# Last layer in pairs of source blocks with clamps on two engines, and another order of the heads' products at the borders of units

## The chip, the core and the metric

The kernel runs on one core of a Trainium2 chip. The metric is device time in microseconds for one execution of the whole program, the median over several runs. TensorE (PE), VectorE (DVE), ScalarE (ACT), GpSimd (POOL) and the DMA queues of SyncE (SP) work side by side and wait for each other through semaphores.

## The reference

Four graph layers run one after the other on x (4096 nodes x 64 features) with one dense 0/1 adjacency matrix (4096 x 4096). Each takes `h = max(layernorm(x), 0)` and adds its result to x.

```python
# layer 0: 6 spatial and 2 intent heads (32 wide), then one output head over their concatenation
e = leaky_relu(f1[:, :, None] + f2[:, None, :], 0.2)          # per head, 4096 x 4096
h_s = elu(softmax(where(adj > 0, e, -9e15)) @ Wh)             # masked attention
# layer 1: hyperbolic attention over neighbours; layer 2: mean of neighbours, W, relu, l2 norm
# layer 3: the last 100 neighbours of each row, halved from one to the one before it
support = h @ weight
mask = adj != 0
rank = cumsum(mask, axis=1);  deg = rank[:, -1:]
k = minimum(deg, 100);  pos = rank - (deg - k)
w = mask * where(pos > 0, 0.5 ** (k - pos), 0.0)
out = w @ support + bias
```

## The kernel before

**Shape of the work.** The adjacency is kept transposed, sources on the 128 partitions and targets along the free axis, so a matrix product with 128 sources (a *block*, 32 of them) adds its part to the sums of many targets. A PSUM bank holds 128 x 512 float32, and most sums are one bank wide. A scheduler orders each engine's instructions from the program's order, its dependences and hints such as `issue_after`.

**The heads (L1443 on).** Targets come in two halves (`hf`) of 2048, and for each half the eight heads (`hd`) are worked through: 16 *units*. The exponential of the leaky sum factors into a source part and a target part once it is known on which side of the leaky relu's corner an edge lies. So a unit needs sign masks, not exponentials. For each pair of blocks `split_edges` makes `st`, the sign of source plus target (one 128x2048 pass per block, most on ACT at L1205, every few on DVE at L1199), then `B = st & edges` (DVE, L1211), and in some pairs `C = B ^ edges` (DVE, L1219); where C is not made, the product with the edges less that with B stands for it.

`add_up` (L1541) multiplies values of 32 columns by four stretches of 512 targets, each landing on its own quarter of the 128 partitions of an accumulator. A spatial head has these accumulators:

- accB: the high half of the values on side B, and accL: their low half, scaled up by LO;
- accD: the denominators;
- accC: the values on the other side.

accB and accC alternate between two pools from one unit to the next, so the next unit's can be started while the last one's are read. accL and accD have one bank each. The two intent heads have no accL; three parts of their values all go to accB. In every pair PE does block by block accB, accL, accD, then accC.

At the end of a unit its sums are evacuated to `ev`: accD by DVE (L1657), accB by ACT (L1658), accC by ACT (L1659), and for spatial heads DVE adds accL/LO (L1661). The rest of the unit's end (`finish_unit`: transposes, division by denominators, elu) is issued at the second pair of the next unit.

**The last layer (L2723 on).** The targets come in four units `u` of 1024. Exponents of the weights come from a product: for each block, `pv` collects a first product with `late` (32 rows deep: how many neighbours lie in later blocks), and a second with `tri` (neighbours within the block, from the fp8 mask `m3`). A relu of `pv` written as int16, read again as bf16 bits, is the weight itself: the clamp (ACT, L2768, 128x1024 in one instruction, `w3b` with three buffers). The products with the support (`sacc`, L2733) of a block come after the `pv` products of the next one. `pv` takes two banks and has two buffers.

Unit 0 is interleaved with the end of the layer before it (four calls of `layer2_group`), whose results are its `SS`, block by block. At a unit's end the two sums are copied out (L2778), turned back by PE (L2783), and added to bias and x (L2791, L2792).

**The check.** The fast form of the kernel is valid for an adjacency of zeros and ones. So every value of it is looked at once: 64 calls of `count_odd` load 128x2048 float32 (1 MB, `raw`, two buffers, on SP's queue) and count the odd ones in one DVE pass (L955). 16 of the 64 are called in the last layer, at every block with `j % 8 == 4`, to be issued after the last `valued`, the last group of the layer before. SP's queue carries the loads of `m3` (512 KB, three buffers) as well.

Of the kernel before, what the change touches and what calls it, by code (L numbers as in the profile page):

```python
# [24 lines left out]
P = 128  # L25
# [810 lines left out]
def kernel(  # L836
# [111 lines left out]

        return col.unsqueeze(2).to_broadcast([P, col.shape[1], width])

    def count_odd(pool, c):

        raw = pool.tile([P, HW], F32, name="raw", tag="raw", bufs=2)
        nc.sync.dma_start(raw, adjT[c % NB * P : (c % NB + 1) * P, c // NB * HW : (c // NB + 1) * HW])
        nc.vector.scalar_tensor_tensor(  # L955
            raw, raw, 0.0, raw, ALU.is_gt, ALU.not_equal, accum_out=bad[:, c : c + 1]
        )
# [83 lines left out]
    with ExitStack() as l0:  # L1041
# [403 lines left out]
        with ExitStack() as ha:  # L1445
# [34 lines left out]
            for hf in range(2):  # L1480
# [9 lines left out]
                for hd in range(NH):  # L1490
# [61 lines left out]
                    for j0 in range(0, NB, 2):  # L1552
                        q = j0 // JT
                        t0 = j0 % JT
                        if spatial:
                            whole = j0 // 2 % 3 > 0
                        else:
                            whole = j0 // 2 % (5 if hf else 2) == 1
                        edges = mres[q][:, t0 : t0 + 2, :]
                        B, C = split_edges(  # L1560
                            epool,
                            srow,
                            nt[:, j0 : j0 + 2, hd],
                            edges,
                            j0 + hd * NB,
                            HEAD_STEPS[not spatial],
                            not whole,
                            3,
                        )
                        if whole:  # L1570
                            C = edges.bitcast(F8)
                        for i, j in enumerate(range(j0, j0 + 2)):
                            for n, (acc, y) in enumerate(parts):
                                sums = add_up(
                                    acc,
                                    y[:, j],
                                    lambda k, i=i: B[:, i, k * G : (k + 1) * G],
                                    start=j == 0 and (n == 0 or acc is not parts[n - 1][0]),
                                    stop=j == NB - 1 and (acc is not accB or n == len(parts) - 2 - spatial),
                                )  # L1580
                        for i, j in enumerate(range(j0, j0 + 2)):
                            for c in range(2):
                                cs = slice(c * O, (c + 1) * O)
                                add_up(
                                    accC,
                                    yc[:, j, cs],
                                    lambda k, i=i: C[:, i, k * G : (k + 1) * G],
                                    start=j == 0 and c == 0,
                                    stop=False,
                                )  # L1590
                                if whole:
                                    add_up(
                                        accC,
                                        ycn[:, j, cs],
                                        lambda k, i=i: B[:, i, k * G : (k + 1) * G],
                                        start=False,
                                        stop=False,
                                    )
                            if first:
                                with behind(sums):  # L1600
                                    add_up(
                                        dm,
                                        YD[:, j].rearrange("p c h -> p (c h)"),
                                        lambda k, q=q, j=j: mres[q].bitcast(F8)[
                                            :, j % JT, k * G : (k + 1) * G
                                        ],
                                        start=(j == 0),
                                        stop=(j == NB - 1),
                                    )
                        if hf == 0 and hd > 0 and j0 % (NB // 2) == 8 and later:  # L1610
                            transfers_after(B.bitcast(U8)[0:1, 0, 0:4], *later.pop(0))
                        if hf == 0 and first and j0 // 2 < NB // 4:
                            with behind(sums, *done_at):
                                other_products(j0 // 2)
                        if hf == 0 and first and j0 == NB // 2:
                            load_products(zt, hd + 1)
                        if j0 >= (NB // 2 + 4 if first else NB // 2 - 4):
                            with behind(*done_at):
                                for _ in range(2 if first else 1):
                                    next(coming, None)  # L1620
                        if j0 == 2 and pending:
                            pending()
                            pending = None
# [23 lines left out]
                    for c in range(2):  # L1647
                        for k in range(NS):
# [5 lines left out]
                                stop=c == 1,  # L1654
                            )
                    ev = by_g
                    nc.vector.tensor_copy(ev[:, 0, :], accD)  # L1657
                    nc.scalar.copy(ev[:, 1, :], accB)  # L1658
                    nc.scalar.copy(ev[:, 2, :], accC)  # L1659
                    if spatial:  # L1660
                        nc.vector.scalar_tensor_tensor(  # L1661
                            ev[:, 1, :], accL, 1.0 / LO, ev[:, 1, :], ALU.mult, ALU.add
                        )

                    def finish_unit(hf=hf, hd=hd, ev=ev, fme=fme):
                        wh = wn[:, hf * HB : (hf + 1) * HB, hd]
# [851 lines left out]
    def layers_fast(es, wide, *sums):  # L2518
# [75 lines left out]
        with not_before_nodes():  # L2594
# [25 lines left out]
            nc.vector.tensor_scalar(w3, w3, Q3[0:D], VAL, ALU.mult, ALU.mult)  # L2620
            fold_3 = lp.tile([P, D], F32, name="fold_3f")
            nc.vector.tensor_scalar(fold_3, fold_h, M3, 2.0**27 / VAL, ALU.mult, ALU.mult)
        late = lp.tile([P, 2, G], BF16, name="late")

        def layer2_group(b0, part, deg):

# [47 lines left out]
        with tc.tile_pool(name="ps_nacc", bufs=6, space=PSUM) as ps_acc:  # L2674
            for hf in range(2):
# [44 lines left out]
                pl = ps.tile([P, G], F32, name="plate", tag="misc")  # L2720
                nc.tensor.matmul(pl, lhsT=lat, rhs=cnt16[:, hf], start=True, stop=True)
                nc.vector.tensor_scalar(late[:, hf], pl, VBITS, None, ALU.min)


        ps_acc = es.enter_context(tc.tile_pool(name="ps_sacc", bufs=2, space=PSUM))
        ps_v = es.enter_context(tc.tile_pool(name="ps_v", bufs=2, space=PSUM))
        for u in range(4):
            hs = slice((u % 2) * HO2, (u % 2 + 1) * HO2)
            accs = [ps_acc.tile([P, G], F32, name="sacc", tag="sacc") for _ in range(NK)]

            def add_up(j, w):
                for k in range(NK):
                    nc.tensor.matmul(  # L2733
                        accs[k],
                        lhsT=SS[:, j].rearrange("p s d -> p (s d)"),
                        rhs=w[:, k * G : (k + 1) * G].bitcast(BF16),
                        start=(j == 0),
                        stop=(j == NB - 1),
                    )

            last = None
            for q in range(NQ):
                m = work.tile([P, JT, HO2], U8, name="m3", tag="m3", bufs=3)
                nc.sync.dma_start(m, mask_d[q][u // 2][:, :, hs])
                for t in range(JT):
                    j = q * JT + t

                    pv = ps_v.tile([P, HO2], F32, name="pv", tag="pv")
                    for k in range(NK):
                        r = ((u % 2) * NK + k) * O  # L2750
                        nc.tensor.matmul(  # L2751
                            pv[:, k * G : (k + 1) * G],
                            lhsT=blk[r : r + O, j, :],
                            rhs=late[r : r + O, u // 2, :],
                            start=True,
                            stop=False,
                        )
                    for k in range(NK):
                        nc.tensor.matmul(  # L2759
                            pv[:, k * G : (k + 1) * G],  # L2760
                            lhsT=tri,
                            rhs=m[:, t, k * G : (k + 1) * G].bitcast(F8),
                            start=False,
                            stop=True,
                        )

                    w = work.tile([P, HO2], I16, name="w3b", tag="w3b", bufs=3)
                    nc.scalar.activation(w, pv, AF.Relu)  # L2768
                    if j % 8 == 4:
                        with tc.issue_after(valued[-1].ins):  # L2770
                            count_odd(work, next(todo))
                    if last is not None:
                        add_up(*last)
                    last = (j, w)
            add_up(*last)
            ev = work.tile([P, NK, G], F32, name="ev3", tag="ev3")
            for k in range(NK):
# [110 lines left out]
```

## Time and profile before

| | |
|---|---|
| median of 3 runs | 2023.15 us (2019.92 to 2024.01) |
| the profiled execution | 2021.7 us |
| its span in the profile | 2019.9 us |
| mean granted TensorE clock | 0.941 |
| heads' stage | about 54 to 930 us |
| ends of the last layer's units (first copy of sums) | 1876.9, 1921.3, 1965.3, 2009.5 us |

The profile is of one execution. A row of the groups reads: line, engine, operation, output from inputs, shapes and count; then busy time, mean ns of one, and the engine's idle time just ahead of them with what ended it. A wait row reads: engine, what waited and its line, what it waited for and its line; then the sum, the number of times, and the longest. PEld is the weight load of TensorE. The clock is the share of full speed that TensorE was granted.

### The profile page before, as it was taken

The numbers are of one execution on the slowest core, as the hardware profiler recorded it, in microseconds if no ns is written. First come the engines' busy times: TensorE is split into PE (matmuls) and PEld (weight loads), VectorE is DVE, ScalarE is ACT, GpSimd is POOL, SyncE is SP. The second block draws the span as 40 slices with busy tenths as digits, with TensorE's granted clock in tenths as the row PEclk, the third lists the DMA queues.
The fourth block names the chain that finished last, engine by engine and source line by source line (L and its number), as shares of the span: only waits on it lengthen the run. The fifth ranks groups of instructions, "written<-read, shape, count | busy, mean of one in ns | idle before, by whom it ended". The sixth has DMA issues, their size and how long they took to land. (4 is left out here: it accounts for less than half of the span.)

```text
span 2019.9 us, 44190 instructions
## 1 busy us (share of the span) xinstructions
PE 1810.5 (90%) x19340; PEld 818.8 (41%) x19340; DVE 1534.4 (76%) x2239; ACT 1474.5 (73%) x1439; POOL 83.4 (4%) x125
## 2 busy tenths in 40 slices
PE   5889989999999999996699958999999985899998
PEld 3444445444444444444244432333333333454332
DVE  6779988998789879996778768888878788533530
ACT  3768888899789888993789857777777743227676
POOL 2000100100000000001011100000000000000000
PEclk8999999999999999997799968999999997889999
DMA  8945564424311111103355415444344336312752
GB/s 112 183 113 100 101 101 65 154 117 172 111 49 49 49 49 54 54 2 96 111 177 194 157 48 199 142 146 153 123 142 150 114 121 221 125 63 73 280 199 65
DMA packets 117016, 239.05 MB, mean 118 GB/s; under 512 B 11062, under 2 KB 84006, under 8 KB 102054
## 3 DMA queue, kind: packets, MB, share of 16 engines
q1 hardware_dynamic: 101996, 192.95, 28.4%
q0 software_dynamic: 14816, 43.18, 11.9%
q8 instruction: 153, 2.51, 0.5%
q14 instruction: 51, 0.42, 0.1%
HBM read 245.37 MB, written 49.46 MB: 146 GB/s over the span
## 5 line engine op out<-in xcount | busy, mean ns | idle before, releaser
L1205 ACT ACTIVATE st<-srow,nt 128x2048 int8<-128x2048 f32 x352 | 682.8, 1994 | 78.4 <-DVE B L1211 77.5
L1211 DVE TENSOR_TENSOR B<-st,mres 128x1024 int32<-128x1024 int32 x256 | 311.7, 1220 | 68.0 <-PE accC L1541 43.5
L1541 PE MATMUL accB<-B,ybh 128*32 128x512 fp8e4 x3072 | 338.7, 384 | 15.6 <-DVE B L1211 15.6
L1541 PE MATMUL accD<-B,ybh 128*32 128x512 fp8e4 x2048 | 301.3, 387 | 21.9 <-DVE h L1657 21.9
L1541 PEld LDWEIGHTS <-ybh 128*32 128x32 bf16 (+1 forms) x6656 | 197.0, 98 | 237.7 <-issue 75.9
L1541 PE MATMUL accC<-B,ycn 128*32 128x512 fp8e4 x2272 | 267.8, 381 | 1.2 <-issue 1.2
L1541 PE MATMUL accC<-mres,ych 128*32 128x512 fp8e4 x2272 | 267.7, 381 | 0.0
L1541 PE MATMUL accL<-B,ybh 128*32 128x512 fp8e4 x1536 | 220.4, 390 | 4.6 <-DVE h L1661 4.5
L1541 PEld LDWEIGHTS <-ych 128*32 128x32 f16 x4096 | 168.7, 98 | 114.5 <-issue 9.1
L1199 DVE TENSOR_SCALAR st<-srow,nt 128x2048 uint8<-128x2048 f32 x160 | 205.4, 1284 | 2.5
L2336 PE MATMUL accj<-sg,who 128*64 128x512 f32 (+1 forms) x512 | 196.6, 614 | 6.5 <-DVE sg L2329 6.1
L2336 PE MATMUL acci<-sg,who 128*64 128x512 f32 (+1 forms) x512 | 196.7, 614 | 0.0
L955 DVE SCALAR_TENSOR_TENSOR raw<-raw 128x2048 f32<-128x2048 f32 x64 | 146.1, 2285 | 33.0 <-DMA raw<-in_adj_dram 32.8
L2292 ACT ACTIVATE yt<-pu,consts 128x512 f32<-128x512 f32 x144 | 98.6, 686 | 98.0 <-PE pu L2291 97.9
L2281 ACT ACTIVATE sg<-pl,rb 128x512 f32<-128x512 f32 x256 | 160.7, 678 | 8.0 <-PE pl L2276 4.9
L2768 ACT ACTIVATE w3b<-pv 128x1024 int16<-128x1024 f32 x128 | 130.9, 1023 | 42.7 <-PE pv L2759 41.2
L1205 ACT ACTIVATE st<-srowo,nto 128x1024 int8<-128x1024 f32 x128 | 138.1, 1137 | 16.4 <-DVE B L1211 14.0
L1541 PE MATMUL accC<-C,ych 128*32 128x512 fp8e4 x1824 | 146.3, 389 | 1.0 <-DVE C L1219 1.0
L1219 DVE TENSOR_TENSOR C<-B,mres 128x1024 int32<-128x1024 int32 x114 | 139.5, 1225 | 3.6
L1541 PEld LDWEIGHTS <-ycn 128*32 128x32 f16 x2272 | 107.7, 97 | 64.2 <-issue 3.6
L2329 DVE SCALAR_TENSOR_TENSOR sg<-pf,sg 128x512 f32<-128x512 f32 x112 | 72.1, 685 | 38.8 <-PE pf L2326 38.8
L2270 PE MATMUL pl<-nm,noid 128*128 128x512 fp8e4 x256 | 82.3, 393 | 13.8 <-ACT sg L2281 12.9
(497 smaller groups left out, 2676.1 us busy)
## 6 DMA issues: line engine op xcount, KB each, us to landing
raw<-in_adj_dram SPq DMA_DIRECT2D x64, 1024.0 KB, 6.2
mo<-edges SPq DMA_DIRECT2D x32, 512.0 KB, 3.9
noedge<-nmo POOLq DMA_DIRECT2D x32, 512.0 KB, 4.1
nm<-noedge SPq DMA_DIRECT2D x64, 256.0 KB, 3.0
m<-edges SPq DMA_DIRECT2D x16, 1024.0 KB, 4.8
m<-edges SPq DMA_DIRECT2D x32, 512.0 KB, 4.9
srow<-srow_d SPq DMA_DIRECT2D x15, 1024.0 KB, 6.8
mres<-in_adj_dram POOLq DMA_DIRECT2D x8, 1024.0 KB, 36.1
```

The lines of the kernel that those rows point to most:

```text
L955: nc.vector.scalar_tensor_tensor(raw, raw, 0.0, raw, ALU.is_gt, ALU.not_equal, accum_out=bad[:, c : c + 1])
L1199: nc.vector.tensor_scalar(st[:, i, :].bitcast(U8), srow, negs[:, i : i + 1], EDGE, ALU.is_gt, ALU.mult)
L1205: nc.scalar.activation(st[:, i, :], srow, AF.Sign, bias=negs[:, i : i + 1], scale=-1.0)
L1211: nc.vector.tensor_tensor(B.bitcast(I32), st.bitcast(I32), edges.bitcast(I32), ALU.bitwise_and)
L1219: nc.vector.tensor_tensor(C.bitcast(I32), B.bitcast(I32), edges.bitcast(I32), ALU.bitwise_xor)
L1541: ins = nc.tensor.matmul(acc[k * O : (k + 1) * O, :], lhsT=values, rhs=moving(k), start=start, stop=stop,)
L2270: nc.tensor.matmul(pl, lhsT=noid, rhs=nm[:, b, :].bitcast(F8), start=True, stop=False)
L2281: nc.scalar.activation(sg[:, b0 + k, :], pl, AF.Sigmoid, bias=rb[:, j : j + 1], scale=1.0)
L2292: nc.scalar.activation(far[gi, gj][:, b, :], pu, AF.Sigmoid, bias=nb_t, scale=2.0 * DIST_K / (DIST_S * DIST_S),)
L2329: nc.vector.scalar_tensor_tensor(v[:, t, :], pf, F_K3, v[:, t, :], ALU.add, ALU.mult)
L2336: nc.tensor.matmul(acc[r : r + n, :], lhsT=XQ[:, src, cols], rhs=w, start=start, stop=stop)
L2768: nc.scalar.activation(w, pv, AF.Relu)
```

## The change

Two parts, in two stages that don't touch each other.

In the heads, a unit other than the very first multiplies its first pair's accB products first, then accC's, and only then accL's and accD's. The last pair does accL and accD for both blocks first, then accB. When a spatial head is evacuated, DVE writes accL/LO to `ev`, copies accD, and adds accB to `ev`; ACT copies accC only. Intent heads are evacuated as before, by the same instructions.

In the last layer two blocks are worked as a pair. The four `late` products of a pair lie on four different row groups of PE: the second block's use `late_x`, a copy of `late` with the two halves of the partitions exchanged (two more DVE passes per half). `pv` becomes four tiles of one bank, with four buffers. The clamp becomes four 128x512 instructions: those with k == 0 on DVE and those with k == 1 on ACT, but in every fourth pair (`j0 % 8 == 4`), which calls the check, all four are on ACT. `w3b` holds a pair and has the pool's own number of buffers. The check is split: its load is now issued one check ahead (`load_rows`), and `check_rows` is called in its old place. The support products of a pair follow the `pv` products of the next pair.

```diff
-    def count_odd(pool, c):
+    def load_rows(pool, c):
         raw = pool.tile([P, HW], F32, name="raw", tag="raw", bufs=2)
         nc.sync.dma_start(raw, adjT[c % NB * P : (c % NB + 1) * P, c // NB * HW : (c // NB + 1) * HW])
+        return raw, c
+    def count_odd(pool, c):
+        check_rows(*load_rows(pool, c))
+    def check_rows(raw, c):
         nc.vector.scalar_tensor_tensor(
             raw, raw, 0.0, raw, ALU.is_gt, ALU.not_equal, accum_out=bad[:, c : c + 1]
         )
...
-                        for i, j in enumerate(range(j0, j0 + 2)):
-                            for n, (acc, y) in enumerate(parts):
-                                sums = add_up(
...
+                        def inside(of_b):
+                            for i, j in enumerate(range(j0, j0 + 2)):
+                                for n, (acc, y) in enumerate(parts):
+                                    if (acc is accB) not in of_b:
+                                        continue
+                                    ins = add_up(
...
+                        if j0 == NB - 2:
+                            inside([False])
+                            sums = inside([True])
+                        elif j0 == 0 and not first:
+                            sums = inside([True])
+                        else:
+                            sums = inside([True, False])
...
+                        if j0 == 0 and not first:
+                            inside([False])
...
                     ev = by_g
+                    if spatial:
+                        nc.vector.tensor_scalar(ev[:, 1, :], accL, 1.0 / LO, None, ALU.mult)
                     nc.vector.tensor_copy(ev[:, 0, :], accD)
-                    nc.scalar.copy(ev[:, 1, :], accB)
+                    if spatial:
+                        nc.vector.tensor_tensor(ev[:, 1, :], ev[:, 1, :], accB, ALU.add)
+                    else:
+                        nc.scalar.copy(ev[:, 1, :], accB)
                     nc.scalar.copy(ev[:, 2, :], accC)
-                    if spatial:
-                        nc.vector.scalar_tensor_tensor(
-                            ev[:, 1, :], accL, 1.0 / LO, ev[:, 1, :], ALU.mult, ALU.add
-                        )
...
                 nc.vector.tensor_scalar(late[:, hf], pl, VBITS, None, ALU.min)
+                for lo, hi in ((slice(0, D), slice(D, P)), (slice(D, P), slice(0, D))):
+                    nc.vector.tensor_scalar(late_x[lo, hf], pl[hi], VBITS, None, ALU.min)
...
-        ps_v = es.enter_context(tc.tile_pool(name="ps_v", bufs=2, space=PSUM))
+        ps_v = es.enter_context(tc.tile_pool(name="ps_v", bufs=4, space=PSUM))
+        rows = load_rows(work, next(todo))
...
-                for t in range(JT):
-                    j = q * JT + t
-                    pv = ps_v.tile([P, HO2], F32, name="pv", tag="pv")
+                for t0 in range(0, JT, 2):
+                    j0 = q * JT + t0
+                    both = [(i, k) for i in range(2) for k in range(NK)]
+                    pvs = {ik: ps_v.tile([P, G], F32, name="pv", tag="pv") for ik in both}
+                    for i, k in both:
+                        r = ((u + i) % 2 * NK + k) * O
                         nc.tensor.matmul(
-                            pv[:, k * G : (k + 1) * G],
-                            lhsT=blk[r : r + O, j, :],
-                            rhs=late[r : r + O, u // 2, :],
+                            pvs[i, k],
+                            lhsT=blk[r : r + O, j0 + i, :],
+                            rhs=(late, late_x)[i][r : r + O, u // 2, :],
...
-                    w = work.tile([P, HO2], I16, name="w3b", tag="w3b", bufs=3)
-                    nc.scalar.activation(w, pv, AF.Relu)
-                    if j % 8 == 4:
+                    w = work.tile([P, 2, HO2], I16, name="w3b", tag="w3b")
+                    for i, k in both:
+                        wk = w[:, i, k * G : (k + 1) * G]
+                        if k == 0 and j0 % 8 != 4:
+                            nc.vector.tensor_scalar(wk, pvs[i, k], 0.0, None, ALU.max)
+                        else:
+                            nc.scalar.activation(wk, pvs[i, k], AF.Relu)
+                    if j0 % 8 == 4:
                         with tc.issue_after(valued[-1].ins):
-                            count_odd(work, next(todo))
+                            check_rows(*rows)
+                            if (u, j0) != (3, NB - 4):
+                                rows = load_rows(work, next(todo))
                     if last is not None:
                         add_up(*last)
-                    last = (j, w)
+                    last = (j0, w)
```

## The prediction

> **What bounds the kernel now.** I read the page's busy table first, then the waits and a timeline of a unit border in the heads' stage, then busy time by stretches, and last the waits of the last layer.
>
> ```profile
> span 2019.9 us, 44190 instructions
> PE 1810.5 (90%) x19340; PEld 818.8 (41%) x19340; DVE 1534.4 (76%) x2239; ACT 1474.5 (73%) x1439; POOL 83.4 (4%) x125
> ```
>
> TensorE is busy 90% of the span, so a gain must be idle PE time, half-clock PE time, or fewer PE passes. The heads run from about 54 to 930 us in 16 units of 52 to 59 us. Waits there (120 to 960 us), each row with its total, count and longest:
>
> ```profile
> DVE B L1211 <- PE accC L1541: 33.5, 35, 2.2
> PE accD L1541 <- DVE h L1657: 21.9, 11, 3.9
> DVE B L1211 <- ACT st L1205: 17.5, 32, 1.7
> PE accL L1541 <- DVE h L1661: 4.5, 5, 3.3
> ```
>
> PE's largest wait, 21.9 us, is for the evacuation copy of accD at a unit's border. The other two rows say that DVE itself mostly waits for PE or ACT, not for its own work. One border, from the timeline (start, duration):
>
> ```profile
> 296.68 1.22 DVE L1211 TENSOR_TENSOR B<-st,mres 128x1024 int32<-128x1024 int32 x1
> 297.94 1.28 DVE L1199 TENSOR_SCALAR st<-srow,nt 128x2048 uint8<-128x2048 f32 x1
> 299.14 0.68 DVE L1657 COPY h<-accD 128x512 f32<-128x512 f32 x1
> 299.88 0.39 PE L1541 MATMUL accD<-B,ybh 128*32 128x512 fp8e4 x2 [2.21 <-DVE h L1657]
> 299.94 0.69 DVE L1661 SCALAR_TENSOR_TENSOR h<-accL,h 128x512 f32<-128x512 f32 x1
> 300.68 0.62 PE L1541 MATMUL accL<-B,ybh 128*32 128x512 fp8e4 x4 [0.41 <-DVE h L1661]
> ```
>
> accB and accC have two buffers each, accL and accD one. PE starts the next unit with one accB product and then stands, since DVE has a sign step of 1.28 us ahead of the copy. Stretches (busy of PE, PEld, DVE, ACT, POOL; PE clock; DMA share; GB/s):
>
> ```profile
> 300.00:304.00 4.00, 3.59 (x38) 1.47 (x39) 3.93 (x4) 4.00 (x3) 0.00 (x0) 0.57 0.18 74
> 780.00:830.00 50.00, 48.70 (x868) 24.01 (x860) 47.38 (x50) 45.30 (x28) 0.00 (x0) 1.00 0.15 55
> 1880.00:1921.00 41.00, 40.91 (x192) 13.26 (x192) 21.03 (x21) 30.70 (x30) 1.57 (x2) 1.00 0.90 323
> ```
>
> After the border the granted clock is 0.57 for 4 us: the stall is paid a second time. In the second half of the heads (780 to 830) DVE is busy 47.4 of 50 us, so what PE gains there DVE can take back. In the last layer PE is busy 40.9 of 41 us, and the DMA share is 0.90. The groups by line there (1880 to 2009 us: busy, mean ns, idle before), and one wait (1830 to 2010 us):
>
> ```profile
> L2768 ACT ACTIVATE w3b<-pv 128x1024 int16<-128x1024 f32 x94 | 96.2, 1023 | 31.6 <-PE pv L2759 31.6
> L2778 DVE COPY ev<-sacc 128x512 f32<-128x512 f32 x2 | 1.4, 688 | 18.9 <-PE sacc L2733 18.9
> L2778 ACT COPY ev<-sacc 128x512 f32<-128x512 f32 x2 | 1.2, 586 | 0.9 <-PE sacc L2733 0.9
> ```
>
> ```profile
> DVE raw L955 <- DMA raw<-in_adj_dram: 29.1, 13, 5.3
> ```
>
> The clamp waits for PE, never the other way; DVE only does checks (16 between 1873 and 1946 us), waits for their transfers, and nobody waits for it.
>
> **The change, heads.** Every unit but the first starts with accB, then accC, and touches accL and accD last; a unit's last pair finishes accL and accD first. For 12 of 16 units (spatial heads) DVE scales accL out by itself, copies accD, and adds accB, where ACT copied accB and DVE added accL. In the changed program's DVE order the two copies stand ahead of the next sign step: the copy comes 1.28 us earlier. On PE the accB products (2 blocks x 4 matmuls) take about 0.43 us and those of accC 0.86 us by the timeline's 0.215 us per four column groups, so accL is needed some 1.1 us later than accD was. The 2.2 us stall at 299 becomes 0 to 0.5 us.
>
> Stalls over all borders, read one by one on PE (3.9 + 1.9, 3.6, 3.3, 2.6, 2.2, 2.8, 0.8, 1.1, 1.1, 3.0, 1.1, 1.7 us), sum to some 26 to 28 us, of which about 24 lie at spatial borders. Half-clock stretches that follow them (191 to 198 us lose 3.4 us, 136 to 144 another 3.4, six others 1.7 each) lose 13.6 us. The ceiling is 40 us. Added: DVE has one more 128x512 PSUM pass per spatial unit, 0.69 us (row L1661, 685 ns), 12 x 0.69 = 8.2 us; ACT loses a copy of 0.56 us. DVE's own instructions in a first-half unit add up to about 49 us (46.0 busy of 50 in 180 to 230), PE's to 47; so once the stall is gone DVE's work sets the unit. I take 2 to 2.4 us for each of 6 first-half borders and 3 us in all for the second half: about -15 us. Bounds: -4 (DVE takes back all but the clock losses at the two worst borders) to -26 (stalls go, clock returns at half of them).
>
> A rule is weighed here. The trace has half clock after PE idled 2.2 us at 299 and 3.6 us at 192, and none after 2.8 us at 411. The Trainium skill, "TensorE: Matmul & The Clock Gate" (Part 1), says the clock halves after an idle window of about 3.4 us, free-running. By a strict 3.4 us the border clock losses would be some 5 us of the 13.6; by the trace, shorter stalls count, with luck in them. I use the trace for what is won, and for new gaps below.
>
> **The change, last layer.** Per pair of blocks before: 2 x (late 0.32 + tri 0.44 + sacc 0.43 + switches 0.09) = 2.57 us; late products start every 1.285 us (1849.10, 1850.39, 1851.68). After: four late products on four row groups at once, 0.32 (before, two on two groups take 0.32), 8 full products x 0.2135 = 1.71, switches 0.09: 2.12 us. If that set the pace, 64 pairs x 0.45 = 29 us would go, 21 in the three units that are not interleaved with the previous layer.
>
> It won't set it alone. The clamp is now four 128x512 instructions. Their prices are in the rows for sacc, the same shape from PSUM: DVE 0.69, ACT 0.59. In three of four pairs DVE has two (1.38), ACT two (1.17); with the products before it and the release after it, the loop through one PSUM bank and DVE is about 0.2 + 1.38 + 0.08 + 0.32 + 0.21 = 2.2 us. In the fourth pair (the check's) ACT has all four: 4 x 0.59 + 0.6 of the same round trip = 2.95. Four pairs: 3 x 2.2 + 2.95 = 9.6 against 10.28 us: -0.7 per four pairs, -2.6 per undisturbed unit.
>
> A rule speaks on this split: "ScalarE: Activation LUTs" (Rules for kernel authors) sends relu and max to VectorE, up to three times faster in bf16. Here the operand is float32 in PSUM, and the rows say 0.69 on DVE against 0.59 on ACT. By the rule a DVE clamp would take about 0.2, and the pair would fall to 2.12 and PE's bound; by the rows it is the slower half. I take the rows.
>
> The checks: 16 of 2.29 us on DVE each, fed by 1 MB transfers that land after 7.6 us (median here; 5.2 at best) through two buffers. Before, DVE waited 29.1 us for them at no cost. Now DVE's program has 2 checks ahead of unit 1, 10 within it, 4 in unit 2, none in unit 3, each with the clamps of later pairs queued behind it. A clamp that stands behind a waiting check stops PE two pairs later, and SP's queue holds mask loads (m3) behind raw loads that wait for an earlier check. With a check every 4.4 to 4.7 us as now, 10 checks alone take 44 to 47 us, against a unit of 44.2 (ends of units 1876.9, 1921.3, 1965.3, 2009.5). A part of the 24 clamps x 0.69 = 16.6 us fits into the waits (13 waits, 29.1 us: 2.2 each), the rest adds. Unit 1: 48 to 56, say +7; unit 2 with 4 checks -1; unit 3 -2.6; unit 0, bound by the chain of the previous layer's four groups (14.8 us each), 0 to +1.5. late_x costs 2 x 2 DVE passes of 64x512 at 0.69 (row of late, 691 ns): 2.8 us, about half on the path, at the start and the end of unit 0, +1.3. No row shows PE gaps of 2 to 4 us there; after such gaps in the heads the clock halved, 1.7 us each: 0 to +5, I take +0.5. Sum: about +5, bounds -12 (checks find their way between clamps) to +13.
>
> **Sum.** -15 + 5 = -10 us. The profiled execution took 2021.7 us (span 2019.9), 1.5 below the median of 2023.15; against the median that is 2013.
>
> **The rivals.**
> 1. The checks decide (slower). One mechanism: in unit 1 DVE meets each check before its transfer landed, and nothing overlaps: 10 x (2.29 + 2.24 wait) + 16.6 of clamps = 62 us against 44, +18, with half clock after some of the gaps +3. With a heads' gain at its low end, -4, that is +17: 2040. It decides as soon as unit 1 is longer than some 59 us, or than 48 if the heads bring only -4. For it: the 29.1 us row and the DMA share of 0.90. Against: clamps do fill waits, and raw loads are issued one check ahead.
> 2. Both parts pay (faster). Heads -28 with most of the clock, last layer -12: 1983. For it: PE is the last wait everywhere. Against: DVE at 47.4 of 50.
> 3. The heads' stall changes its name: PE waits for B where it waited for accD, DVE's 8.2 us more are paid, heads -4, last layer +3: 2022, no change. For it: the DVE rows of 780 to 880 us. Against: DVE waited 33.5 us for PE over the stage.
> 4. The scheduler leaves the DVE copies behind the sign step in some units: heads -8, as in 3 otherwise. The written order speaks against it.
>
> **How the numbers follow.** A few runs tell no change to about 0.2%, 4 us. Forecast 0.55 (2003 to 2019, at 2013), rival 2 0.17 (1978 to 2000), rivals 3 and 4 0.15 (2016 to 2027), rival 1 0.13 (2027 to 2045). The range 1995 to 2027 leaves out about 0.2. Faster 0.73, same 0.13, slower 0.14.
>
> **What would show it.** Heads: the waits of PE for accD and accL, 26 us together, fall below 8; no half clock at 191 or 300 us; DVE B <- PE accC shrinks and PE accB <- DVE B grows if DVE takes over. Last layer: DVE waits on raw within unit 1, PE on w3b there; unit 1 above 46 us, unit 3 near 41. I am wrong if unit 1 is no longer than before, or if the heads' units keep their length.

## The result, and the profile after

The changed kernel took 2025.12 us in the median of 22 runs (2021.37 to 2033.89), the kernel before 2023.09 beside it: a ratio of 1.0012, interval 1.0002 to 1.0023. The forecast was 2013. Its profiled execution has a span of 2023.3 us against 2019.9. The page's first rows, of the changed kernel:

```profile
span 2023.3 us, 44268 instructions
PE 1803.8 (89%) x19323; PEld 821.9 (41%) x19340; DVE 1602.9 (79%) x2351; ACT 1426.4 (71%) x1459; POOL 83.4 (4%) x125
```

PE is busy 6.7 us less in a span that is 3.4 us longer: it waits some 10 us more than before. The heads' stage ends (last accD copy) at 931.7 us instead of 929.1. In the last layer, from the last `pnf` product of the layer before (1855.1 us, before 1858.1) to the last unit's first copy of sums (2012.2, before 2009.5), it takes 157.1 us instead of 151.4: +5.7.

**Heads.** The waits of the changed kernel from 120 to 960 us, some of its rows:

```profile
DVE B L1218 <- PE accC L1548: 33.2, 39, 2.2
PE pt L1699 <- DVE rd L1716: 30.9, 13, 3.5
DVE B L1218 <- ACT st L1212: 14.3, 27, 1.7
PE accL L1548 <- DVE h L1680: 3.1, 3, 1.5
```

and accD's row in the groups:

```profile
L1548 PE MATMUL accD<-B,ybh 128*32 128x512 fp8e4 x2048 | 288.8, 387 | 1.6 <-DVE h L1681 1.6
```

The waits for accD and accL fell from 26.4 to 4.7 us, as meant. A new one, 22.8 us longer than it was, stands at the top of PE's: `pt <- rd`, 30.9 us, against 8.1 before:

```profile
PE pt L1676 <- DVE rd L1693: 8.1, 8, 2.1
```

These are the third set of transposes in `finish_unit`. The `misc` tiles of PSUM have two buffers; the third `pt` takes the first one's, and must wait until DVE's sums `rd` have read it. The border at 299 us of before, in the changed kernel (timeline of DVE and PE; start and duration):

```profile
294.60 0.68 DVE L1680 TENSOR_SCALAR h<-accL 128x512 f32<-128x512 f32 x1
295.20 0.68 DVE L1681 COPY h<-accD 128x512 f32<-128x512 f32 x1
295.80 0.68 DVE L1683 TENSOR_TENSOR h<-h,accB 128x512 f32<-128x512 f32 x1
...
299.93 1.22 DVE L1218 TENSOR_TENSOR B<-st,mres 128x1024 int32<-128x1024 int32 x1
301.18 1.23 DVE L1226 TENSOR_TENSOR C<-B,mres 128x1024 int32<-128x1024 int32 x1
302.32 1.22 DVE L1218 TENSOR_TENSOR B<-st,mres 128x1024 int32<-128x1024 int32 x1
303.45 0.20 DVE L1714 TENSOR_REDUCE rd<-pt 128x16 f32<-128x48 f32 x1
```
```profile
295.94 0.40 PE L1548 MATMUL accD<-B,ybh 128*32 128x512 fp8e4 x4 [0.19 <-DVE h L1681]
...
299.72 1.09 PE L1699 MATMUL pt<-ident,h 128*128 128x128 f32 x8
...
303.92 0.63 PE L1699 MATMUL pt<-ident,h 128*128 128x128 f32 x4 [2.35 <-DVE rd L1716]
```

The border itself costs PE 0.19 us instead of 2.6. Four microseconds later PE has made two sets of transposes, runs a few products on, and stands 2.35 us at the third set: DVE's queue has B, C and B ahead of the sum that frees the tile. Over the whole stage PE's idle time did not shrink, and its mean clock did not rise. Here is the stretch from the first to the last accD copy, before and after (columns as in the prediction):

```profile
135.06:929.13 794.07, 752.51 (x12799) 373.89 (x12802) 707.62 (x778) 684.95 (x420) 25.51 (x33) 0.98 0.30 78
134.77:931.71 796.94, 750.85 (x12769) 370.47 (x12773) 713.70 (x790) 680.65 (x407) 25.52 (x33) 0.97 0.30 78
```

PE is idle 41.6 us of it before and 46.1 after.

**Last layer.** The first copies of sums of the units are at 1873.9, 1925.4, 1971.0 and 2012.2 us: units 1 to 3 take 51.4, 45.7 and 41.2 us, against 44.4, 44.0 and 44.2. DVE in unit 1 and at the start of unit 2, where clamps (L2798) stand behind checks (L962):

```profile
1894.60 2.28 DVE L962 SCALAR_TENSOR_TENSOR raw<-raw 128x2048 f32<-128x2048 f32 x1
1896.81 0.08 DVE L962 DVE_READ_ACCUMULATOR raw<-raw 128x1 f32 x1
1898.41 2.29 DVE L962 SCALAR_TENSOR_TENSOR raw<-raw 128x2048 f32<-128x2048 f32 x1 [1.51 <-DMA raw<-in_adj_dram]
1900.62 0.08 DVE L962 DVE_READ_ACCUMULATOR raw<-raw 128x1 f32 x1
1900.62 1.28 DVE L2798 TENSOR_SCALAR w3b<-pv 128x512 int16<-128x512 f32 x2
```
```profile
1939.61 2.29 DVE L962 SCALAR_TENSOR_TENSOR raw<-raw 128x2048 f32<-128x2048 f32 x1 [2.73 <-DMA raw<-in_adj_dram]
1941.83 0.08 DVE L962 DVE_READ_ACCUMULATOR raw<-raw 128x1 f32 x1
1941.83 1.28 DVE L2798 TENSOR_SCALAR w3b<-pv 128x512 int16<-128x512 f32 x2
```
```profile
1942.56 0.38 PE L2778 MATMUL pv<-late_x,LDf 32*128 32x512 bf16 x1 [2.76 <-DVE w3b L2798]
```

Two checks in a row and a wait for the second one's transfer hold DVE from 1894.6 to 1900.6; at 1939.6 a wait of 2.73 us and a check come before the next clamp, and PE stands 2.76 us.

### The profile page after: what moved, and what is told of

Read it like the earlier page. It is cut to its first block, busy times and chain, and to the rows that moved or that the text cites. A ratio compares the mean times of both kernels' runs of the same rounds, so it can differ in the third digit from the quotient of the medians.

```text
span 2023.3 us, 44268 instructions
## 1 busy us (share of the span) xinstructions
PE 1803.8 (89%) x19323; PEld 821.9 (41%) x19340; DVE 1602.9 (79%) x2351; ACT 1426.4 (71%) x1459; POOL 83.4 (4%) x125
## 5 line engine op out<-in xcount | busy, mean ns | idle before, releaser
L1548 PE MATMUL accB<-B,ybh 128*32 128x512 fp8e4 x3072 | 326.2, 384 | 12.7 <-DVE B L1218 12.7
L1548 PE MATMUL accD<-B,ybh 128*32 128x512 fp8e4 x2048 | 288.8, 387 | 1.6 <-DVE h L1681 1.6
L1548 PE MATMUL accL<-B,ybh 128*32 128x512 fp8e4 x1536 | 212.4, 386 | 3.1 <-DVE h L1680 3.1
L962 DVE SCALAR_TENSOR_TENSOR raw<-raw 128x2048 f32<-128x2048 f32 x64 | 146.0, 2283 | 12.7 <-DMA raw<-in_adj_dram 12.6
L2800 ACT ACTIVATE w3b<-pv 128x512 int16<-128x512 f32 x160 | 87.0, 596 | 78.4 <-PE pv L2786 41.1
L2798 DVE TENSOR_SCALAR w3b<-pv 128x512 int16<-128x512 f32 x96 | 62.7, 685 | 48.5 <-PE pv L2786 41.6
```

The costliest lines, as they stand in the source:

```text
L962: nc.vector.scalar_tensor_tensor(raw, raw, 0.0, raw, ALU.is_gt, ALU.not_equal, accum_out=bad[:, c : c + 1])
L1548: ins = nc.tensor.matmul(acc[k * O : (k + 1) * O, :], lhsT=values, rhs=moving(k), start=start, stop=stop,)
L2798: nc.vector.tensor_scalar(wk, pvs[i, k], 0.0, None, ALU.max)
L2800: nc.scalar.activation(wk, pvs[i, k], AF.Relu)
```

## The experiments

Each kernel was timed beside the kernel before (2023 us). "Alone" means the other stage is as before.

**1. The two parts alone.** heads_only and last_only take the diff's lines of one stage each.

> Heads' part alone, last layer as before. Theory A (the stall at a unit's border only changes its place: PE no longer waits for accD and accL, 26 us before, but for the third set of transposes of finish_unit, which needs DVE's two sums rd): heads' stage as long as before within 3 us, waits of PE pt for rd 25 us or more, time 2020 to 2026. Rival B (the heads do gain, and the last layer ate it): accD and accL waits gone, stage shorter by 8 us or more, time 2008 to 2015.

2020.8 us, ratio 0.9979 (0.9965 to 0.9993): theory A's waits, at theory A's time (`pt <- rd` 29.4 us; accD and accL 4.7). The stage ends at 924.8, 4 us earlier, one more than theory A allowed. From the first to the last accD copy:

```profile
134.43:924.81 790.38, 745.82 (x12768) 367.28 (x12772) 713.24 (x789) 680.49 (x407) 25.50 (x33) 0.98 0.30 79
```

PE is idle 44.6 us, no less than before, and the clock is 0.98, as before.

> Last layer's part alone, heads as before. Theory A: all of the loss is here: unit 1 about 51 us long against 44, unit 2 some 46, unit 3 41, together +4 to +7 us: 2026 to 2031. Rival B would need the same loss or more here, +8 to +15 us, 2031 to 2038, so that the two parts sum to the +2 measured.

2026.5 us, ratio 1.0016 (1.0001 to 1.0030). Unit 1 takes 53.7 us, unit 2 43.6, unit 3 41.2. So the loss is in unit 1, and theory A holds, at its low end.

**2. finish_unit two pairs later.** On heads_only:

```diff
-                        if j0 == 2 and pending:
+                        if j0 == 6 and pending:
```

> heads_only with finish_unit called at the fourth pair (j0 == 6) of the next unit and not at the second (j0 == 2), so that DVE has two more pairs to catch up after the border. Theory A1 (DVE is only late for a moment after the border): PE's waits of pt for rd fall from some 30 to below 10 us and the heads' stage gets shorter by 8 to 18 us, time 2006 to 2016. Rival A2 (DVE's and ACT's own work sets the pace of a unit): the wait goes but comes back as PE waiting for B or C, stage within 4 us of heads_only, time 2019 to 2027.

2020.0 us, ratio 0.9987 (0.9976 to 0.9998). Its PE waits, from 130 to 960 us:

```profile
PE pt L1692 <- DVE rd L1709: 31.1, 14, 4.2
```

A1 fell in the form in which it was stated: the wait is as long two pairs on. So it isn't that DVE is late only for a moment after the border; the wait came at both places where the third set was asked for right behind the first two. The time lies in A2's range, but A2's wait for B or C didn't come.

**3. finish_unit in two steps.** On heads_only, with no instruction added: the third set is asked for at the next pair.

```diff
-                        if j0 == 2 and pending:
-                            pending()
-                            pending = None
+                        if j0 == 2 and pending:
+                            next(pending)
+                        if j0 == 4 and pending:
+                            for _ in pending:
+                                pass
+                            pending = None
...
+                        yield
                         pt = by_block(2)
```

> heads_only with finish_unit in two steps: its first two sets of transposes at the second pair of the next unit as before, the third set (the one for which PE waits until DVE has read the first, 29.4 us in 13 waits) at the third pair (j0 == 4). No instruction is added or taken away. Theory A1 (the wait is only an order in which PE asks too early): PE's waits of pt for rd below 8 us, heads' stage shorter than in heads_only by 10 to 20 us, time 2001 to 2011. Theory A2 (DVE sets the length of a unit: it is busy 49.9 of 51.1 us in the unit from 190 us): the wait shrinks, others grow (PE for B, accB or C), stage within 5 us of heads_only, time 2016 to 2026.

2010.6 us, ratio 0.9942 (0.9923 to 0.9961): -11.7 us. Its PE waits, 130 to 960 us:

```profile
PE tr L1000 <- DVE x L1732: 15.0, 4, 5.7
...
PE pt L1695 <- DVE rd L1712: 8.0, 7, 4.5
PE accB L1541 <- DVE B L1211: 7.7, 13, 1.3
PE pf L1648 <- ACT h L1644: 6.4, 2, 4.7
PE accC L1541 <- DVE C L1219: 5.6, 9, 1.0
PE accL L1541 <- DVE h L1676: 4.0, 4, 1.5
...
PE accD L1541 <- DVE h L1677: 2.1, 7, 0.6
```

The stage ends at 919.1, ten us earlier than before, with the same passes on DVE as in heads_only. Against heads_only it is -0.37%, 7 to 8 us. The time lies in A1's range, at its end, though the gain in the stage is below A1's 10 to 20 us. A2 fell for the stage as a whole, but not for every unit: the one from 190 us takes 51.0 us in heads_only with DVE busy 49.8, and 50.8 here with the same 49.8. A part of the wait went to B and C (13.3 us together, against 3.9 in heads_only over the same stretch). From the first to the last accD copy:

```profile
134.53:919.13 784.60, 742.66 (x12769) 377.80 (x12772) 711.63 (x790) 679.13 (x407) 24.96 (x33) 0.98 0.30 79
```

PE is idle 41.9 us, 2.7 less than in heads_only. The other 3.1 us by which this stretch is shorter are busy time; PE's clock from 130 to 510 us was 0.97 in heads_only and 0.99 here. So waiting that went is about half of what the profiles show of the gain.

**4. Fewer sign passes on DVE.** On heads_only, the sign passes of pairs j0 = 4 and 20 of a spatial unit go to ACT:

```diff
-                if (n + i) % step == step - 1:
+                if (n + i) % step == step - 1 and not all_act:
...
+                            spatial and j0 in (4, 20),
```

> heads_only with the sign passes of two pairs (j0 = 4 and 20) of each spatial unit all on ACT: 1.33 passes of 1.28 us less on DVE per unit, 1.33 of 2.00 us more on ACT. Theory A2 (DVE sets the length of a unit, 49.9 of 51.1 us busy, with ACT at 45.3): spatial units get shorter by 0.5 to 1.7 us, stage by 6 to 18 us, time 2003 to 2015. Rival A1 (an order of waits, not DVE's work): no change in the stage within 4 us; rival A3 (ACT is as near to its limit as DVE, by its waits for B): stage longer by 3 to 12 us, 2024 to 2033.

2030.8 us, ratio 1.0045 (1.0031 to 1.0059): A3. DVE's waits, 130 to 960 us:

```profile
DVE B L1211 <- ACT st L1205: 38.3, 56, 2.2
```

Against 14.9 us in heads_only: DVE waits for the passes that ACT now does, 23.4 us more. That says nothing clean of A2, since what DVE was relieved of came back as waits for ACT.

**5. The split without the change, and the order without the evacuation.** before_split has experiment 3's split on the kernel before. order_split is heads_split with the old evacuation put back:

```diff
-                    if spatial:
-                        nc.vector.tensor_scalar(ev[:, 1, :], accL, 1.0 / LO, None, ALU.mult)
                     nc.vector.tensor_copy(ev[:, 0, :], accD)
-                    if spatial:
-                        nc.vector.tensor_tensor(ev[:, 1, :], ev[:, 1, :], accB, ALU.add)
-                    else:
-                        nc.scalar.copy(ev[:, 1, :], accB)
+                    nc.scalar.copy(ev[:, 1, :], accB)
                     nc.scalar.copy(ev[:, 2, :], accC)
+                    if spatial:
+                        nc.vector.scalar_tensor_tensor(
+                            ev[:, 1, :], accL, 1.0 / LO, ev[:, 1, :], ALU.mult, ALU.add
+                        )
```

> The kernel before with only finish_unit in two steps, as in heads_split: the old product order and the old evacuation stay. Theory A1 (PE has one slack to lose at each border: it was taken by the wait for accD, and where that went, by the wait for rd): here the border's 22 us for accD stay and only the 8.1 us of waits for rd go, part of them: heads' stage shorter by 0 to 6 us, time 2016 to 2024. Rival E (the split alone is worth what heads_split brought, the product order nothing): 2008 to 2014.

2014.3 us, ratio 0.9966 (0.9949 to 0.9982): 2 us below A1's range and 0.3 above rival E's. Its profiled execution shows the old wait in full and the other one gone:

```profile
PE accD L1541 <- DVE h L1660: 22.8, 11, 3.9
PE tr L1000 <- DVE x L1716: 10.2, 4, 5.7
PE accL L1541 <- DVE h L1664: 4.6, 7, 3.3
PE pf L1633 <- ACT h L1629: 3.0, 2, 1.5
...
PE accB L1541 <- DVE B L1211: 2.7, 4, 1.3
PE pt L1679 <- DVE rd L1696: 2.1, 1, 2.1
PE accC L1541 <- DVE C L1219: 2.0, 4, 0.7
```

That execution took 2021.9 us, 7.5 more than the median, so its stage (it ended at 927.5, 1.6 us earlier than before) doesn't show where the gain came from. By the times the two parts simply add up: the split is worth some 0.34% on the old order and 0.9942 / 0.9979, 0.37%, on the new one, and 0.9979 x 0.9966 is 0.9945, as much as both together brought. So A1 is not borne out: the split brings as much where it takes 6 us of `pt <- rd` (8.1 to 2.1) as where it takes 21 (29.4 to 8.0), and what it does beyond that wait stays open. E isn't refuted either: on top of the split the new order and evacuation are worth 0.9942 / 0.9966, 0.24%, but the two intervals overlap.

The waits show where the stall's time went even with the split. From 130 to 960 us PE waits 21.3 us less for accD and accL in heads_split than here (6.1 against 27.4), and longer elsewhere: 5.9 us for `pt`, 4.8 for `tr`, 5.0 for accB, 3.6 for accC and 3.4 for `pf`, 22.7 together. (`tr` and `pf` are other products of PE at the ends of units, which wait for tiles of DVE and ACT.)

> heads_split with the evacuation of before (accD by DVE, accB by ACT, then accL added by DVE) under the new order of products. Theory F (the new evacuation is needed: accL's bank is free only after ACT's copy of accB, which stands behind a sign pass of 2.0 us): PE waits for accL and accD 10 to 25 us in all, time 2013 to 2020. Rival G (the product order alone gives PE the time it needs): waits below 6 us, time 2008 to 2013, and up to 3 us better than heads_split since DVE has 8.2 us less to do.

2023.7 us, ratio 1.0007 (0.9994 to 1.0019): theory F's waits for accL and accD, 25.4 us, with a time 4 us above its range.

```profile
PE accL L1541 <- DVE h L1679: 24.9, 8, 4.7
```

With ACT's copy of accB in between, accL's bank comes free late, and the new order waits for it as long as the old one waited for accD. The order and the evacuation belong together, and the 8.2 us of DVE passes that the evacuation adds are well spent.

**6. The checks kept in their pairs.** On last_only; `issue_after` keeps order on DVE and adds no wait.

```diff
                         if k == 0 and j0 % 8 != 4:
-                            nc.vector.tensor_scalar(wk, pvs[i, k], 0.0, None, ALU.max)
+                            clamped = nc.vector.tensor_scalar(wk, pvs[i, k], 0.0, None, ALU.max)
...
-                        with tc.issue_after(valued[-1].ins):
+                        with tc.issue_after(valued[-1].ins), tc.issue_after(clamped.ins):
                             check_rows(*rows)
```

> last_only with each check kept behind the last DVE clamp ahead of its own pair, in DVE's order (no wait added). The order then has one check per six DVE clamps in units 1 to 3, where last_only has ten checks in unit 1. Theory C (crowded checks in DVE's queue cost unit 1 its 7 us): unit 1 at 42 to 45 us, units 2 and 3 at 41 to 43, last layer 3 to 8 us shorter than before: 2015 to 2020. Rival D (two clamps of 0.69 us on DVE and 0.59 on ACT are too slow for the pair wherever the checks stand): unit 1 falls to about 46 at best, units 2 and 3 get longer by what it loses, time 2022 to 2028.

2017.0 us, ratio 0.9968 (0.9957 to 0.9979): theory C. The units take 45.3, 41.2 and 41.2 us (42 to 45 said for unit 1). Windows of the two last units:

```profile
1921.60:1962.80 41.20, 40.27 (x210) 15.20 (x208) 26.49 (x37) 21.98 (x41) 1.50 (x2) 1.00 0.63 212
1962.80:2004.00 41.20, 40.27 (x209) 15.22 (x208) 26.87 (x39) 22.01 (x42) 1.86 (x3) 1.00 0.42 139
```

PE is busy 40.3 of 41.2 us again, and DVE 26.5 us with four checks in each. The checks are the same, and their transfers too; only their places in DVE's queue differ.

**7. All clamps on ACT.** On last_only: `if k == 0 and j0 % 8 != 4:` becomes `if False:`.

> last_only with all four clamps of every pair on ACT (the checks stay where the scheduler puts them, with no clamp behind them in DVE's queue). By the trace of the changed kernel four clamps on ACT take 2.06 us in a row and a pair that has them 2.9 us on PE. Theory C (the checks in front of DVE's clamps made unit 1 long): unit 1 falls from 51 to 46 to 47, as long as units 2 and 3, which get longer: 16 pairs x 2.9 = 46; last layer about 6 us longer than before, time 2027 to 2031. Rival D (the pair form itself, not the checks, made unit 1 long): unit 1 stays above 49.

2032.6 us, ratio 1.0057 (1.0041 to 1.0072), somewhat slower than said. Unit 1 falls from 53.7 to 46.0 us, as theory C has it; units 2 and 3 take 48.2 each, a pair 3.0 us. The timeline, one pair:

```profile
1992.17 2.06 ACT L2784 ACTIVATE w3b<-pv 128x512 int16<-128x512 f32 x4 [0.84 <-PE pv L2770]
1992.56 1.03 PE L2744 MATMUL sacc<-w3b,XAf 128*128 128x512 bf16 x4
1993.52 0.39 PE L2762 MATMUL pv<-late,LDf 32*128 32x512 bf16 x2
1993.80 0.86 PE L2762 MATMUL pv<-late_x,LDf 32*128 32x512 bf16 x2
1994.59 1.04 PE L2770 MATMUL pv<-m,tri 128*128 128x512 fp8e4 x4
1995.08 2.06 ACT L2784 ACTIVATE w3b<-pv 128x512 int16<-128x512 f32 x4 [0.84 <-PE pv L2770]
```

The next `late_x` waits for a bank that ACT empties last. So the pairs on four row groups gain nothing without DVE's share of the clamps.

**8. Together.** both_pinned is the changed kernel with experiment 6; both_split_pinned has experiments 3 and 6.

> The changed kernel with each check kept behind the last DVE clamp ahead of its pair, as in last_pinned. If the two parts do not touch each other, the heads' -4 (heads_only) and the last layer's -6.5 (last_pinned) add up: 2010 to 2015. If they do (the heads' clock or the DMA load shift the last layer), 2016 to 2020.

2016.5 us, ratio 0.9966 (0.9955 to 0.9977). No more than last_pinned alone: the heads' part in its written form added nothing here, as it added nothing to last_only (1.0012 against 1.0016). Whether its 0.2% in heads_only was more than luck stays open. In the profiles unit 1 took 48.6 us here, at a clock of 0.89, and 45.3 in last_pinned, at 0.96, with the same code in this stage; that is more than the 2 us by which the stretch between the accD copies is shorter here (793.7 against 795.7).

> The changed kernel with finish_unit in two steps and the checks pinned: -11.7 of heads_split and -6.5 of last_pinned if they add up: 2003 to 2008; if part is lost in other stages, as with both_pinned, 2008 to 2012.

2006.0 us, ratio 0.9922 (0.9894 to 0.9949): -17 us. The two gains, 0.9942 x 0.9968 = 0.9910, add up within the interval; unit 1 took 48.7 us in its profile, as in both_pinned. It beats both kernels.

## Why the prediction was wrong, point by point

- **Heads, the border.** Right: the accD and accL waits, forecast below 8 us, are 4.7; the copies stand ahead of the sign pass and accL is late by nothing much.
- **Heads, the sum (-15 us).** Wrong, and it is the step that failed: "I take 2 to 2.4 us for each of 6 first-half borders and 3 us in all for the second half". It took the stall that goes as time gained, nearly one for one, and did not ask what PE needs from DVE next. That was the third set of transposes, some 4 us on. In the trace of before it was a row of 8.1 us. It grew to 30.9, +22.8 us, against the 21.7 that accD and accL lost. So PE waited as long as before in all (idle 41.6 us of the stage before, 44.6 in heads_only, 46.1 in the changed kernel), and heads_only gained 0.2%, 4 us. Experiment 3 took most of the new wait away and brought -11.7 us in all, but that isn't the forecast gain come late: the split alone brings 0.34% to the kernel before, and the new order and evacuation are worth some 4 to 5 us by the ratios, with it as without it. With the split the stall's 21 us reappear in five smaller waits (experiment 5). Why PE's waits add up to the same again is not shown.
- **Heads, two sums.** The stalls listed add up to 29.1 us, not 26 to 28, and the half-clock losses to 17.0, not 13.6 (3.4 + 3.4 + 6 x 1.7). Both would have made the ceiling higher, so they are not the cause of the miss.
- **Heads, the reason given for caution.** "DVE's work sets the unit" was right for some units, such as the one from 190 us (DVE busy 49.8 of 51.0 us in heads_only and of 50.8 in heads_split), and not for others: the next one fell from 53.7 to 51.6 us with the split and the same DVE passes. PE's waits for B did not take the stall's place, as rival 3 had it; that rival had the result nearly right, by another wait.
- **Heads, the clock.** Of the two places named, the half clock at 191 us went (185 to 205 us: 0.83 before, 1.00 after). The one at 300 us stayed (296 to 310 us: 0.88 in both); it now came behind the new stall, which ended at 303.9. The mean of 0.97 against 0.98 can't be put down to the change: heads_only and both_pinned run the same code in the heads at 0.98.
- **Last layer (+5).** Right in sign and size, 5.7, with some luck in the sum: unit 1 +7.0 (said +7), unit 3 -3.0 (said -2.6), but unit 2 +1.7 (said -1), while nothing is seen of the +1.3 for late_x and of unit 0's 0 to 1.5 (18.8 us from the last `pnf` product to its first copy, before and after). The four `late` products take 0.32 us together as said, and a pair of the undisturbed unit 2.16 us (said 2.2). By experiments 6 and 7 the checks hoisted into unit 1 are the cause in last_only (53.7 us; 45.3 with the checks held back, 46.0 with no clamp on DVE). In the changed kernel holding them back took unit 1 only from 51.4 to 48.6 us, and no run shows what the rest comes from.
- **ScalarE or VectorE for the clamp.** The rows of the changed kernel are 685 ns on DVE and 596 on ACT, and four in a row on ACT take 2.06 us, 0.515 each. So for float32 from PSUM the trace stands against the rule on relu that the prediction weighed; the rule's factor is for bf16, and no clamp here reads bf16.
- **Rival 1** (unit 1 of 62 us) was too dark: the clamps do fill waits; DVE waited for raw transfers 9.4 us in all from 1830 to 2010 us, not 29.1.

```profile
DVE raw L962 <- DMA raw<-in_adj_dram: 9.4, 8, 2.7
```

## What to carry to other kernels

When a change takes away a stall between two engines, follow the late engine to its next request of the other one, and read how many passes that one has queued ahead of the answer; a small wait further on can be small only because of the stall ahead of it. Then add up the waiting engine's idle time over the whole stage: twice here some 21 us left one row and came back in others. Where tiles of a short ring are asked for in a row, put independent work of the asking engine between the last free tile and the first one that must come back. And where an engine gets a share of a paced loop, look at what the scheduler has placed in its queue: work that nobody waited for, like the checks, must be held in the slots that were planned for it.

## What the runs showed of the hardware

Executions of unchanged stages differ by the clock that TensorE is granted. The stretch from 932 to 1800 us has the same code in all kernels; before and after:

```profile
932.00:1800.00 868.00, 752.86 (x4412) 310.53 (x4410) 660.38 (x1197) 564.95 (x773) 35.98 (x55) 0.91 0.43 144
```
```profile
932.00:1800.00 868.00, 750.50 (x4466) 311.33 (x4459) 664.03 (x1210) 566.40 (x776) 38.44 (x58) 0.92 0.43 144
```

A hundredth of the clock over 868 us is some 9 us of full-speed time, and the changed kernel made up 5.5 us between the end of the heads (2.6 us late) and the first `pnf` product of the second half (1806.45 us, before 1809.39: 2.9 early). That is more than the change moved the total. The heads vary too: the same code took 790.4 us from the first to the last accD copy in heads_only, 793.7 in both_pinned and 796.9 in the changed kernel. So a stage's length in one execution says little by itself.
